# The last batch's first expert layer in two levels of seven products, with its factors streamed

## The chip, the cores and the metric

The kernel runs on one core of one Trainium2 chip, all in fp32. The metric is device microseconds (us) of one execution; three runs of the kernel before gave a median of 3222.79.

## The reference

`x` holds 4 batches of 2048 tokens of width 512. First comes a windowed attention with a layer norm before and after it, then a feed-forward layer whose weights are mixed per batch out of 8 experts:

```python
x = x + layernorm(attention(layernorm(x), w_qkv))      # windows of 128, 16 heads of 32, 3 windows of keys
h = layernorm(x)
# per batch of 2048 tokens here (the reference's own B, S, H, F, E names are kept)
g   = (relu(h @ gate_w1.T + gate_b1) @ gate_w2.T + gate_b2).mean(over the batch's tokens)   # 8 numbers
mW1 = W1 + sum_e g[e] * TW1[e]      # 2048 x 512
mW2 = W2 + sum_e g[e] * TW2[e]      # 512 x 2048
u   = gelu(h @ mW1.T + mb1)
out = x + layernorm(u @ mW2.T + mb2)
```

## The kernel before

The program runs in two stages. In the attention stage (up to about 1672 us) it walks 64 windows, and beside them it computes the gates. In the feed-forward stage it walks 16 blocks (`K`) of 512 tokens; batch `b` = K // 4, so blocks 12 to 15 are the last batch, called `DEEP`.

*Seven products for eight.* Both feed-forward layers cut each matrix into a 2 x 2 grid and compute 7 products of quarter matrices in place of 8 (Strassen's scheme in Winograd's form), with sums of the factors made before and sums of the results after. The names `A11, A12, S1, S2, S4, S3, A22` are the seven left factors made from the weights; the right factors come from the tokens.

- *First layer.* A block has four sets (`begin`, `middle`, `end`, c = 0, 2, 4, 6: two 128-row tiles of hidden units above and two below). Each set computes the seven products (`product`, L1023) into PSUM banks `X`, `Z`, `Y`, with 256 tokens as columns. The factors of a batch stay in SBUF for its four blocks (`w1_of`, loaded by `load_first` from `m1_d`).
- *Second layer.* `second` (`product2`, L1143) does the same with factors that are streamed from DRAM (`m2_d`) through six buffers `w2s` by `load_second`. For the last batch only, `second_deep` goes down one level more: each of the seven outer products is itself done as seven inner products (`inner`, L1308) of 128 columns, 49 in place of 64. The inner left factors come from `m3_d`. The inner right factors (`inner_right`) are made on DVE by `inner_sums` (four subtractions of 512 per outer product, L1233), one outer product ahead. Results go from PSUM to `y` by DVE adds (L1270) or ACT copies. POOL makes the outer right factors t1, b12 and t2 from the GELU results (L1105, L1106, L1111), and t3 at outer product 4 (L1345).
- *Mixing.* `mixer` is a generator (`blend`) that is advanced by hand at chosen places (`steps`, `next(blend)`). One step loads one expert's piece (512 KB, `exps`) three steps ahead and adds it into an accumulator on DVE (`scalar_tensor_tensor`, L155); after eight experts four DVE operations make the sums (L163 to L166), and stores put the factors into DRAM. It goes through batches, layers, eight chunks and eight experts in order, 576 steps in all. `inner_mixer` afterwards makes the inner sums of the last batch's second layer in 14 steps; it is advanced in block 11's second layer and in block 12's first.

How many steps each place takes is set by hand:

```python
step = mixing(*((2, 1, 1, 1) if c == 2 else (1, 1, 1, 1)))    # a set of the first layer
products2 = second(K, before, mixing(3, 2, 3, 2, 2, 3, 2), load_x1)
```

The order on each engine is the order of the program, and DMAs are issued from SP's queue, also in order. [...]

Of the kernel before, what the change touches and what calls it, by code (L numbers as in the profile page):

```python
# [34 lines left out]
def sandwich(ctx: ExitStack, tc: tile.TileContext, x, w_qkv, gw1, gb1, gw2, gb2, w1, b1, w2, b2, tw1, tb1, tw2, tb2, out):  # L35
# [23 lines left out]
    gw1_sb = const.tile([P, KC, D], F32, name="gw1_sb")  # L59
# [16 lines left out]
        for b in range(NB)  # L76
# [6 lines left out]
    m3_d = {b: dram.tile([P, 7, 8, PAIRS2, P], F32, name=f"m3d_{b}") for b in DEEP}  # L83
# [3 lines left out]
    order_deep = [A11, S1, A12, S3, S2, S4, A22]  # L87

# [17 lines left out]
    def mixer():  # L106

        todo = [(b, s, c, e) for b in range(NB) for s in range(2) for c in range(HC) for e in range(NX)]
        ets, accs = {}, {}
# [5 lines left out]
        def load(n):  # L115
            b, s, c, e = todo[n]
            base, exps = ((w1, tw1), (w2, tw2))[s]
            if e == 0:
                acc = mix.tile([P, 2, D], F32, tag="acc", name=f"acc_{b}_{s}_{c}")
                nc.sync.dma_start(acc, halves(base)[c])  # L120
                accs[b, s, c] = acc
            et = mix.tile([P, 2, D], F32, tag="exps", bufs=4, name=f"exps_{b}_{s}_{c}_{e}")
            nc.sync.dma_start(et, halves(exps[e])[c])
            ets[n] = et

        def store(b, s, c, acc, sums):
            rows = acc.rearrange("p h (q d) -> p h q d", d=Q)
            if s == 0:
# [5 lines left out]
            elif b in DEEP:  # L134
                for i, at in enumerate(((0, 7), (3, 6))[c % 2]):
                    cols = slice(i * P, (i + 1) * P)
                    nc.sync.dma_start(m3_d[b][:, A11 : A12 + 1, at, c // 2, :], rows[:, :, 0, cols])
                    nc.sync.dma_start(m3_d[b][:, S1 : S4 + 1, at, c // 2, :], sums[:, :, cols])
                    nc.sync.dma_start(m3_d[b][:, S3 : A22 + 1, at, c // 2, :], rows[:, :, 1, cols])
# [5 lines left out]
        for n in range(3):  # L145
            load(n)
        yield
        for n, (b, s, c, e) in enumerate(todo):
            if n + 3 < len(todo):
                load(n + 3)  # L150
            for f in late:
                f()
            late = []
            acc = accs[b, s, c]
            nc.vector.scalar_tensor_tensor(acc, ets.pop(n), g_all[b][:, e : e + 1], acc, ALU.mult, ALU.add)  # L155
            yield
            if e == NX - 1:
                del accs[b, s, c]
# [10 lines left out]
        for f in late:  # L169
            f()  # L170

    issued = {b: 0 for b in DEEP}

    def inner_mixer(b):

        todo = [(o, h) for o in order_deep for h in range(2)]
        loaded, late = {}, []

        def load(n):
            o, h = todo[n]  # L180
            two = slice(2 * h, 2 * h + 2)
            et = mix.tile([P, 4, 2, P], F32, tag="exps", bufs=4, name=f"inner_{b}_{o}_{h}")
            nc.sync.dma_start(et[:, :2], m3_d[b][:, o, 0:8:7, two, :])
            nc.sync.dma_start(et[:, 2:], m3_d[b][:, o, 3:7:3, two, :])
            loaded[n] = et

        def store(n, et):
            o, h = todo[n]
            two = slice(2 * h, 2 * h + 2)
            nc.sync.dma_start(m3_d[b][:, o, 1, two, :], et[:, 3])  # L190
            nc.sync.dma_start(m3_d[b][:, o, 2, two, :], et[:, 0])
            nc.sync.dma_start(m3_d[b][:, o, 4:6, two, :], et[:, 1:3])
            issued[b] = n + 1

        for n in range(2):
            load(n)
        yield
        for n in range(len(todo)):
            for f in late:
                f()  # L200
            if n + 2 < len(todo):
                load(n + 2)
# [1403 lines left out]
```

## Time and profile before

| | |
|---|---|
| median of three runs | 3222.79 us (3222.3 to 3224.71) |
| the profiled execution | 3220.89 us, span 3219.1 us |
| busy: PE, DVE, ACT, POOL | 3195.0, 2283.2, 1578.2, 676.9 us |
| blocks 1 to 11 of the feed-forward stage | 96.7 us each |
| blocks 12, 13, 14 | 94.0, 93.0, 93.1 us |
| block 15 and the end | 104.5 us |
| mean granted TensorE clock | 0.999 |

PE is the matmul engine, PEld its weight loads, DVE the vector engine, ACT the scalar engine, POOL GpSimd, SP the engine that issues the DMAs. In a row of the windows view the numbers are the stretch, its length, then the busy time of each engine with its instruction count, the granted clock, the DMA share and GB/s. A row of the timeline gives the start, the time taken (of all that are merged in it), the engine, the line and the operation; in brackets stands how long the engine was idle before, and what ended that. A row of waits reads: who waited for whom, us in total, times, longest. A matmul of fp32 appears as two instructions.

### The profile page before, as it was taken

What the parts mean: (1) busy time and instruction counts of PE and PEld (TensorE: products, weight loads), DVE (VectorE), ACT (ScalarE), POOL (GpSimd) and SP (SyncE); (2) the same over time, 40 slices, a digit from 0 to 9 for tenths busy, and PEclk for the clock granted to TensorE, in tenths of its full rate; (3) what the DMA queues carried; (4) which work ended last, traced back from release to release, by engine and by line L of the source; (5) the groups of instructions that cost most, each with busy time, mean ns of one, the idle gap of its engine ahead of it and who ended that gap; (6) DMA issues with size and microseconds to landing.
All of it is one profiled execution on the core that took longest, in us unless ns stands there. A gap on an engine that the chain in (4) does not pass through costs nothing.

```text
span 3219.1 us, 61654 instructions
## 1 busy us (share of the span) xinstructions
PE 3195.0 (99%) x23862; PEld 2695.0 (84%) x23862; DVE 2283.2 (71%) x3307; ACT 1578.2 (49%) x4332; POOL 676.9 (21%) x847
## 2 busy tenths in 40 slices
PE   9999999999999999999999999999999999999998
PEld 7788878788787887878768888888888888889998
DVE  5766666888998889888865665677757667554555
ACT  3777777777777777777761222112222112222222
POOL 0111111111111111110112332323322333322222
PEclk9999999999999999999999999999999999999999
DMA  2111112455555556554677889998999999874555
GB/s 87 52 59 54 41 60 80 134 185 170 195 194 164 176 176 202 192 183 149 213 276 277 310 308 346 359 336 326 313 329 364 336 328 321 305 248 162 193 187 171
DMA packets 363334, 688.88 MB, mean 214 GB/s; under 512 B 27161, under 2 KB 115353, under 8 KB 357026
## 3 DMA queue, kind: packets, MB, share of 16 engines
q1 hardware_dynamic: 363042, 684.94, 61.5%
q8 instruction: 189, 3.10, 0.4%
q14 instruction: 103, 0.84, 0.1%
HBM read 567.39 MB, written 117.44 MB: 213 GB/s over the span
## 4 chain that ended last, share of the span: by engine, by line
PE 95%; DVE 3%; DMA 1%; ACT 0%; POOL 0%; issue 0%; SPq 0%; POOLq 0%; DVEq 0%; ACTq 0%
PE pm L518 23%; PE px L1023 13%; PE ptp L686 11%; PE px L1143 7%; PE sc L649 7%; PE pz L1023 6%; PE po L707 5%; PE pz L1143 5%; PE py L1023 3%; PE px L1308 3%; PE py L1143 3%; PE py2b L1143 2%; PE pz L1308 1%; PE pm L582 1%; PE ptx L340 1%; PE pto L311 1%
## 5 line engine op out<-in xcount | busy, mean ns | idle before, releaser
L155 DVE SCALAR_TENSOR_TENSOR acc<-exps,g,acc 128x1024 f32<-128x1024 f32 x512 | 697.6, 1362 | 65.9 <-DMA exps<-in_tw 59.5
L658 DVE TENSOR_REDUCE nm<-sc 128x2 f32<-128x768 f32 (+1 forms) x512 | 449.1, 918 | 204.9 <-PE sc L649 199.9
L671 ACT ACTIVATE pr<-sc,nm 128x384 f32<-128x384 f32 (+1 forms) x1024 | 573.5, 593 | 11.1 <-DVE nm L658 11.0
L691 ACT COPY prT<-ptp 128x512 f32<-128x512 f32 x732 | 382.7, 594 | 278.7 <-PE ptp L686 278.3
L686 PEld LDWEIGHTS ptp<-ident,pr 128*128 128x128 f32 x2944 | 316.9, 140 | 102.0 <-issue 89.5
L686 PE MATMUL ptp<-ident,pr 128*128 128x128 f32 x2944 | 377.6, 277 | 0.0
L1060 ACT COPY py<-px 128x512 f32<-128x512 f32 x63 | 36.0, 571 | 661.4 <-PE px L1023 661.4
L1023 PE MATMUL px<-tT,w 128*128 128x256 f32 x1512 | 350.0, 379 | 0.6 <-DVE cpv L1083 0.6
L1023 PEld LDWEIGHTS px<-tT,w 128*128 128x128 f32 x1512 | 286.8, 190 | 40.1 <-DVE cpv L1083 1.0
L649 PE MATMUL sc<-k,q 32*128 32x384 f32 (+2 forms) x2816 | 242.8, 422 | 3.9 <-ACT pr L671 3.7
L671 ACT ACTIVATION_READ_ACCUMULATOR pr<-sc,nm 128x1 f32 x1024 | 236.3, 231 | 0.0
L1080 DVE TENSOR_TENSOR cpb<-pz,cpb 128x512 f32<-128x512 f32 x63 | 43.4, 689 | 268.6 <-PE pz L1023 239.0
L96 POOL TENSOR_SCALAR ve_b<-mv_b 128x1 f32<-128x1 f32 x64 | 42.9, 670 | 816.9 <-DVE mv_b L94 816.9
L707 PEld LDWEIGHTS po<-prT,v 128*32 128x32 f32 x5888 | 152.2, 110 | 50.9 <-ACT pr L671 24.6
L707 PE MATMUL po<-prT,v 128*32 128x128 f32 x5888 | 189.7, 275 | 0.2
L649 PEld LDWEIGHTS sc<-k,q 32*128 32x128 f32 x2816 | 118.4, 183 | 74.8 <-issue 53.7
L1143 PE MATMUL px<-w2s,u 128*128 128x256 f32 x784 | 175.1, 379 | 0.0
L1105 POOL TENSOR_TENSOR t<-u 128x512 f32<-128x512 f32 x60 | 81.7, 1362 | 433.9 <-ACT u L1035 433.9
L518 PE MATMUL pm<-xnT,wqkv 128*128 128x256 f32 x720 | 172.0, 382 | 0.0
L1143 PEld LDWEIGHTS px<-w2s,u 128*128 128x128 f32 x784 | 149.0, 190 | 20.3
L518 PEld LDWEIGHTS pm<-xnT,wqkv 128*128 128x128 f32 x720 | 132.0, 190 | 16.6
L1074 ACT COPY cpb<-px 128x512 f32<-128x512 f32 x63 | 36.9, 586 | 181.6 <-PE px L1023 181.6
(295 smaller groups left out, 5914.4 us busy)
## 6 DMA issues: line engine op xcount, KB each, us to landing
exps<-in_tw SPq DMA_DIRECT2D x512, 512.0 KB, 6.2
w2s<-m2d SPq DMA_DIRECT2D x168, 512.0 KB, 8.0
w2s<-m3d SPq DMA_DIRECT2D x84, 512.0 KB, 4.8
acc<-in_w SPq DMA_DIRECT2D x64, 512.0 KB, 6.5
x<-in_x SPq DMA_DIRECT2D x64, 256.0 KB, 4.0
m1d<-acc SPq DMA_DIRECT2D x64, 256.0 KB, 6.5
w<-m1d SPq DMA_DIRECT2D x16, 1024.0 KB, 7.7
fxT<-xTd SPq DMA_DIRECT2D x16, 1024.0 KB, 8.6
```

The costliest lines, as they stand in the source:

```text
L155: nc.vector.scalar_tensor_tensor(acc, ets.pop(n), g_all[b][:, e : e + 1], acc, ALU.mult, ALU.add)
L518: nc.tensor.matmul(bank[u not in chain][:, half, :], lhsT=a[:, kc, ts(half, P)], rhs=b[:, kc, :], start=(u not in (2, 3, 4) and half == kc ...
L649: nc.tensor.matmul(scs[r // 2][:, r % 2, col : col + nj * W], lhsT=q[rows, g, ts(W_ % WB, W)], rhs=k_of[kb][rows, g, j0 * W : (j0 + nj) * ...
L658: nc.vector.tensor_reduce(st["nm"][:, h : h + 2], scs[u][:, :, : nk * W], AX.X, ALU.max, negate=True)
L671: nc.scalar.activation(pr[:, : nk * W], scs[r // 2][:, r % 2, : nk * W], AF.Exp, bias=st["nm"][:, h : h + 1], accum_out=st["den"][:, h : h ...
L686: nc.tensor.transpose(pt[:, r, :], st["pr"][g * 4 + r][:, ts(j, W)], ident)
L691: nc.scalar.copy(prT, pt)
L707: nc.tensor.matmul(po[r * E : (r + 1) * E, n, :], lhsT=v_of[kb][:, jj, h * E : (h + 1) * E], rhs=prT[:, r, :], start=(j == 0), stop=(j == ...
L1023: nc.tensor.matmul(bank[:, f, :], lhsT=factor[:, f, kc * P : (kc + 1) * P], rhs=right[:, kc, :], start=(start and f == 0 and kc == 0), sto ...
L1105: nc.gpsimd.tensor_tensor(t1s[c], b12, us[c][:, :, :Q], ALU.subtract)
L1143: nc.tensor.matmul(bank[:, t, :], lhsT=right(c - c % 2)[:, c % 2, ts(t, P)], rhs=w[:, c % (HC // 2), :], start=(start and c == 0 and t == ...
L1308: nc.tensor.matmul(bank, lhsT=right(p), rhs=w[:, p, :], start=(start and p == 0), stop=True, skip_group_check=True,)
```

## The change

1. The last batch's first layer is computed in two levels too (`first_deep`): 7 outer products, each of 7 inner ones, with 128 weight rows as the stationary operand and 128 tokens as columns. The three inner-factor sets of outer products 1, 3 and 5 (`KEPT`) stay in SBUF for the batch; those of 0, 2, 4 and 6 are streamed again in every block through the six `w2s` buffers. The results of an outer product are added into the four blocks c11, c12, c21, c22 of the hidden matrix in SBUF, by DVE, ACT or POOL; GELU follows in place as a block is complete. `close`, called in the second layer's outer product 0, ends the last one and issues the last 12 GELUs and the eight POOL operations for b12 and t2.
2. The tokens' inner sums (`token_sums`) are made on DVE: part 0 for the next block at outer product 4 of the second layer, part 2 after product 0, part 1 after product 1. The first sums of the second layer (`prepare(0)`) are made after product 3 of the first.
3. Mixing follows a written plan (`mixing_plan`). For the second layer of batches 2 and 3 each expert piece is loaded once and added into two accumulators; batch 3's lie in the place of the gate weights, which are split into two tiles for that. The inner sums of both layers (28 steps) are part of the plan, loaded two steps ahead. Everything ends after product 1 of block 11's second layer. A chunk's stores are issued before the next load, not after it.
4. The step counts per set and product change, and `load_second` doesn't reach into the next block until that block's first layer has begun (`wanted`): two loads at each of the sets 2, 4 and 6.

```diff
+    order_first = [A11, A12, S2, S1, S4, S3, A22]
+    KEPT = (1, 3, 5)
...
+        def chunk(batches, k, c, between=()):
+            waiting = [x for x in todo if x[0] == "later"]
+            for e in range(NX):
+                todo.append(("mix", batches, k, c, e))
+                if e == 1 and waiting:
+                    todo.remove(waiting[0])
+                    todo.append(("sum", *waiting[0][1:]))
+            todo.append(("sum", batches[0], k, c))
+            for b in batches[1:]:
+                todo.append(("later", b, k, c))
+            todo.extend(("inner", *x) for x in between)
...
+        for b, k in ((0, 0), (0, 1), (1, 0), (1, 1), (2, 0)):
+            for c in range(HC):
+                chunk((b,), k, c)
+        for c in range(HC - 1):
+            chunk((2, 3), 1, c)
+        chunk((2,), 1, HC - 1)
+        chunk((3,), 1, HC - 1)
+        for c in range(HC):
+            chunk((3,), 0, c, again[1][2 * c - 2 : 2 * c] if c else ())
+        todo.extend(("inner", *x) for x in again[0])
...
+        def token_sums(K, part):
...
+            src, to = (
+                (xT.rearrange("p (i k) t -> p i k t", k=2)[..., :Q], xsum_of[K, 1][:, :, :2]),
+                (xT[:, 2:, Q:].unsqueeze(1), xsum_of[K, 1][:, :, 2:]),
+                (tT_of[K], xsum_of[K, 0]),
+            )[part]
+            g11, g12, g21, g22 = (src[:, :, k, j * P : (j + 1) * P] for k in range(2) for j in range(2))
+            a, b, c, d = (to[:, i] for i in range(4))
+            for args in ((a, g12, g11), (b, g22, a), (c, g22, g12), (d, g21, b)):
+                nc.vector.tensor_tensor(*args, ALU.subtract)
...
+            plan = [(c12, None), (c11, c12), (c21, c12), (c22, None), (c12, c12), (c21, c21), (c21, c21)]
...
+            def inner(j, n, bank, right, start=False):
+                w = weights_first(K, j, n)
+                for p in range(PAIRS2):
+                    nc.tensor.matmul(bank[:, p, :], lhsT=w[:, p, :], rhs=right, ...)
+
+            def emit(at, bank, out, other):
+                if other is None:
+                    nc.scalar.copy(out(at), bank)
+                else:
+                    add(out(at), bank, other(at))
...
+            def extra(j, at, engine):
+                if j == 3:
+                    add(c12(at), c21(at), c22(at), engine)
+                elif j == 5:
+                    add(c22(at), c22(at), c21(at), engine)
+
+            def tail(j, X):
+                right = tokens[j][1][:, 3, tokens[j][2]]
+                inner(j, 6, X, right)
+                released(j, 3)
+                emit((1, 0), X, *plan[j])
+                extra(j, (1, 0), nc.gpsimd if j == 3 else nc.vector)
...
+            for j in range(7):
...
+                inner(j, 0, X, raw(0, 0), True)
+                nc.scalar.copy(Y, X)
+                inner(j, 1, Z, sums[:, 0, at], True)
+                released(j, 0)
+                emit((1, 1), Z, out, other)
+                if tails:
+                    tails.pop()()
+                if j == 6:
+                    for c in range(0, HC, 2):
+                        nc.gpsimd.tensor_tensor(
+                            t1s["all"][:, c // 2], us[c][:, :, Q:], us[c][:, :, :Q], ALU.subtract
+                        )
+                inner(j, 2, X, sums[:, 1, at])
+                emit((0, 1), X, out, other)
+                gelu_some(j, 4)
+                inner(j, 3, Y, raw(1, 0))
+                released(j, 1)
+                emit((0, 0), Y, out, other)
+                extra(j, (0, 0), nc.gpsimd)
+                gelu_some(j, 2 if j < 6 else 0)
+                inner(j, 5, Z, raw(1, 1))
+                add(out((0, 1)), Z, out((0, 1)))
+                extra(j, (0, 1), nc.gpsimd)
+                gelu_some(j, 2 if j < 6 else 0)
+                inner(j, 4, X, sums[:, 2, at])
+                released(j, 2)
+                add(out((1, 1)), X, out((1, 1)))
+                extra(j, (1, 1), nc.vector)
+                if j == 0:
+                    token_sums(K, 2)
+                if j == 1:
+                    token_sums(K, 1)
+                if j == 3:
+                    next(products2)
+                tails.append(lambda j=j, X=X: tail(j, X))
+                yield
+
+            def close():
+                tails.pop()()
+                for f in (*acts[6], *gelus(K, 1, 0)):
+                    f()
+                for c in range(0, HC, 2):
+                    p, b12, b22 = c // 2, us[c][:, :, Q:], us[c + HC][:, :, Q:]
+                    nc.gpsimd.tensor_tensor(b12, b22, b12, ALU.subtract)
+                for c in range(0, HC, 2):
+                    p, b22 = c // 2, us[c + HC][:, :, Q:]
+                    nc.gpsimd.tensor_tensor(t2s[p // 2][:, p % 2], b22, t1s["all"][:, p], ALU.subtract)
...
@@ second_deep
+                if o == 4 and not last_block:
+                    token_sums(K + 1, 0)
...
                 if o == 0:
-                    end(*closing)
+                    closing.pop()()
...
@@ the loop over blocks
-                elif K == 0 or (k == NBLK - 1 and b + 1 < NB):
-                    step = mixing(0, 1, 0, 1)
+                elif k == NBLK - 1 or K == 0:
+                    step = mixing(*((0, 1, 0, 1) if K in (0, 11) else (1, 1, 1, 1)))
                 else:
-                    step = mixing(*((2, 1, 1, 1) if c == 2 else (1, 1, 1, 1)))
-                if K // NBLK in DEEP and k == 0:
-                    step = lambda: next(inner, None)
+                    step = mixing(*((2, 1, 1, 1) if c == 2 or (c == 4 and PAIRED <= K < 2 * NBLK) else (1, 1, 1, 1)))
...
+                counts = (3, 3, 3, 3, 3, 3, 3) if PAIRED <= K < 2 * NBLK else (3, 2, 3, 2, 2, 3, 2) if b < 2 else (2,) * 7
+                products2 = second(K, before, mixing(*counts), load_x1)
...
+                if K + 1 == DEEP[0] * NBLK:
+                    if j == 1:
+                        assert next(blend, 0) == 0
+                    if 1 < j < 5:
+                        load_kept(j - 2)
+                    if j == 5:
+                        token_sums(K + 1, 0)
```

## The prediction

> **What bounds the kernel now.** I read the page's busy line first, then TensorE's waits in the last four blocks (those of batch 3, the only batch whose matmuls change), then their windows, the chain, and the timeline around one block's second layer.
>
> ```profile
> PE 3195.0 (99%) x23862; PEld 2695.0 (84%) x23862; DVE 2283.2 (71%) x3307; ACT 1578.2 (49%) x4332; POOL 676.9 (21%) x847
> ```
>
> ```profile
> PE px L1308 <- DVE y L1270: 1.5, 5, 0.8
> ```
>
> ```profile
> 2834.50:2928.50 94.00, 92.97 (x617) 86.53 (x617) 61.88 (x123) 24.97 (x59) 27.73 (x27) 1.00 0.72 249
> 2928.50:3021.50 93.00, 92.79 (x618) 86.54 (x617) 46.70 (x97) 24.98 (x59) 27.02 (x30) 1.00 0.50 173
> ```
>
> ```profile
> 2860.37 1.73 PE py L1023 x8
> ...
> 2889.41 1.79 PE px L1308 x16
> ```
>
> TensorE (PE) is busy for 99% and waits for others for 1.5 us in the last 385 us. So time goes only if PE has less to do, and comes back if PE is made to wait. The windows are blocks 12 and 13 (us, PE, PEld, DVE, ACT, POOL, clock, DMA share, GB/s). The chain gives both matmul prices: eight 256-column instructions take 1.73 us (the first layer, L1023), eight 128-column ones 1.79/2 = 0.893 us (the second layer by eighths, L1308).
>
> The price of waiting stands in the timeline, DVE then POOL:
>
> ```profile
> 2883.47 1.76 DVE L1233 TENSOR_TENSOR inner_right<-u 128x512 f32<-128x512 f32 x1
> 2885.15 1.75 DVE L1233 TENSOR_TENSOR inner_right<-u,inner_right 128x512 f32<-128x512 f32 x1
> 2887.03 0.27 DVE L1270 TENSOR_TENSOR y<-px,mb 128x128 f32<-128x128 f32 x1
> 2888.76 0.68 DVE L1233 TENSOR_TENSOR inner_right<-t 128x512 f32<-128x512 f32 x1
> 3002.49 2.69 DVE L1233 TENSOR_TENSOR inner_right<-t,inner_right 128x256 f32<-128x256 f32 x2
> ```
>
> ```profile
> 2883.17 1.51 POOL L1105 TENSOR_TENSOR t<-u 128x512 f32<-128x512 f32 x1 [1.90 <-ACT u L1035]
> 2884.76 1.60 POOL L1106 TENSOR_TENSOR u<-u,u 128x512 f32<-128x512 f32 x1
> 2886.32 1.72 POOL L1111 TENSOR_TENSOR t<-u,t 128x512 f32<-128x512 f32 x1
> 3000.61 5.71 POOL L1345 TENSOR_TENSOR u<-u,t 128x512 f32<-128x512 f32 x4 [18.65 <-PE pz L1308]
> ```
>
> The same DVE operation, 512 wide with both inputs in SBUF, takes 0.68 us alone and 1.75 while POOL works: it stands until POOL's operation (1.27 alone) has ended. One that reads PSUM (2887.03) isn't held. A 256-wide pair at 3002.49 took 2.69 instead of 0.75.
>
> **The PE term.** The first layer of a block is 4 sets x 7 products x 8 instructions: 28 x 1.7275 (6.91 us for 32 in the chain) = 48.4 us. By eighths it is 49 groups of 8 at 0.893 = 43.8. That is 4.6 less per block, 18.4 in four. Both layers ideally take 92.1 now; block 13 takes 93.0, so 0.9 is lost already (the junction of the layers, and the fifth outer product). I keep it. Block 12 loses 1.0 more, where the inner sums still run in its first layer; these now end in block 11: -1.0.
>
> **DVE's work.** The new first layer has 34 adds of 512 from PSUM for 8 now (0.69 each: +17.9), 3 SBUF adds (+2.1) and the token sums, four each of 512, 256 and 128 (0.69, 0.42 by the weight sums' row, 0.28: +5.6). DVE goes from 46.7 to 72 us of some 92: not the bound by its sum. But it works in order, and PE needs certain adds within one product (7 groups, 6.25 us). So I walked one block's queues by hand, each operation at the duration above:
>
> 1. Products 3 to 4. Behind product 3's last add DVE has one extra add and the four sums for the second layer's first product, 0.69 + 4 x 0.65 = 3.3 us, before it can empty product 4's Z bank (0.69). With 0.2 to reach DVE and 0.6 for the add itself that is 4.8 us; PE comes back to Z after 5 groups, 4.5 us. Stall 0.3. POOL meanwhile runs three extra adds; each that comes in between holds DVE for up to 1.27, so up to 2.4. I take 1.4: between the ends, one hold.
> 2. Product 6. POOL's four differences for t1 (5.1 us) stand beside a DVE extra add that is ahead of the add freeing X. 0 to 1.0; I take 0.6.
> 3. Second layer, outer products 0 and 1. Now three POOL operations fall here (2883.17 to 2888.04); after the change eight do (b12 and t2 of all four pairs, 10.2 us), since all the last GELUs come at the end. The next eight inner sums of DVE stand beside them, four at 1.7 instead of 0.65: +4.2 us. Of that some 3 are covered, as sums are made one outer product ahead. 0 to 2.5; I take 1.0.
> 4. Outer product 4, in blocks 12 to 14. Four token sums (256 wide) are put ahead of this product's adds, exactly where POOL's four L1345 operations run and where PE already stalls now:
>
> ```profile
> 3005.84 1.16 PE L1308 MATMUL px<-w2s,inner_right 128*128 128x128 f32 x8 [0.18 <-DVE y L1270]
> ```
>
> Alone they are 4 x 0.33 = 1.3 us, and one hold of about 1 us more before POOL ends at 3006.3. There is no slack, so 2.0 goes to PE. From 0.5 (DVE catches up behind it) to 5.0 (each held at 1.3, as at 3002.49).
>
> These are the edits that speak against the saving. [...]
>
> **Edits with no cost, and their cover.** *Mixing.* 39 DVE steps in blocks 4 to 6 instead of 34, 5 x 1.45 = 7 us more on 66 to 70 busy of 96.7; 33 and 37 instead of 25 in blocks 3 and 7, 12 to 17 more on 54. PE there waits for nobody, and each bank's add has a product (6.9 us) to come. If that cover fails, up to 1 us in each of four blocks; a gain is excluded beyond the 1.9 us of PE waits in blocks 1 to 11. *Loads.* 56 expert loads of 512 KB fall away in the pairs (29 MB); the streamed factors add 4 x 7 tiles of 256 KB per block, also 29 MB. That is 7.3 MB per block of some 92 us, +80 GB/s on 173 at a DMA share of 0.50, about block 12's 249 GB/s at 0.72, which held PE up in no row. Six tiles are ahead (over 10 us of PE) and land in 4.8. They share SP's queue with the output stores, which wait for DVE's adds at products 1 and 2; the same lead covers that, and the kept product 1 reads no stream. *Stores ahead of loads.* In the mixer SP now waits for the weight sums (4 x 0.42 to 0.67 us) before the next load; three loads are ahead, so DVE at worst waits where PE doesn't. *Block 11 to 12.* The last inner sums, kept loads and first token sums end in block 11's second layer, where DVE has 47.1 us of work in 96.7; 0 to 3 us. *Split gate weights.* The same matmuls; nothing.
>
> **The sum.** Against the profiled execution's span of 3219.1: -18.4 - 1.0 + 4 x (1.4 + 0.6 + 1.0) + 3 x 2.0 = -1.4, so 3217.7. The execution's own time is 3220.89, 1.8 above its span, and the median of the runs 3222.79, 1.9 above that: 3217.7 + 3.7 = 3221.4, say 3221. With all unknowns at their low ends: -19.4 + 4 x 0.3 + 3 x 0.5 = -16.7, to 3206; if the 0.9 per block went too, 3203. At their high ends, with the mixing's 4 and the 3 at block 12: -19.4 + 4 x 5.9 + 3 x 5 + 7 = +26, to 3249.
>
> **The rivals.** *PE keeps most of its saving* (0.36): the holds fall on POOL or into DVE's idle 20 us per block. At 0.5 each for items 1 to 3 and 1.0 for item 4: -19.4 + 6 + 3 = -10.4, 3212. For it: DVE is far from full, and a hold of 1.2 is less than two groups. Against: at 3005.84 one hold already reached PE. *The port decides against it* (0.19): the eight POOL operations and the token sums cost their bounds, 2.5 and 5.0, the rest as taken: -19.4 + 4 x 4.5 + 3 x 5 = +13.6, 3236. It ends slower once the new stalls pass 19.4/4 = 4.9 us per block, and by over 0.2% from (19.4 + 6.4)/4 = 6.5. For it: the three operations in the rows stretch two sums to 1.75. Against: in block 12 that stretch alone cost PE no wait in any row. *The blend isn't ready* (0.05): block 12 waits for its streamed or kept factors, one load chain of store, load and sum, three times 5 to 6 us: 3221 + 10 to 15. *Stalls eat the saving* (0.40) is the forecast.
>
> **How the numbers follow.** 0.2% (6.4 us) is about what a measurement of this kernel can tell from no change. The forecast case lies within it; the first rival is faster; the other two are slower: 0.36, 0.40, 0.24. The forecast case's own range is 3216 to 3228. The range of 8 in 10 takes in most of the first rival and part of the second, 3207 to 3235.
>
> **What would show it.** Matmuls at L1023 down by 896 (4 x 4 x 56), and 1568 new ones of 128 columns at 0.893 us per eight; if these cost more, the PE term is wrong. Blocks 12 to 14 at 92 to 95 us and 15 at 90 to 92 of PE; 88 to 90 each would be the first rival, 96 or more the second. PE waits on DVE of about 3 us per block in the first layer's products 4 and 6 and the second's outer products 1 and 4, with DVE operations at 1.2 to 1.8 us beside POOL's; if PE waits but DVE is not beside POOL there, the cause is DVE's order alone. Blocks 1 to 11 at 96.7 each; longer, and the mixing isn't free. A PE wait on DMA at w2s would make the load reasoning wrong.

## The result: 1.1% slower, and the profile after

The changed kernel took 3258.95 us (3255.42 to 3262.51) against 3223.11 us for the kernel before on the same chip, a ratio of 1.0111 [1.0093, 1.0128]. The predicted 3221 (3207 to 3235) is missed by 38 us. The profiled execution of after took 3262.51 us, span 3260.7, 41.6 more than before's 3219.1. Where the 41.6 lie, by the starts of the blocks' first matmuls:

| part | before | after | difference |
|---|---|---|---|
| up to block 0 | 1672.6 | 1674.2 | +1.6 |
| blocks 0 to 2 | 290.6 | 291.7 | +1.1 |
| block 3 | 96.7 | 106.1 | +9.4 |
| blocks 4 to 7, each | 96.7 | 96.7 | 0 |
| blocks 8, 9, 10 | 96.7, 96.7, 97.6 | 103.5, 103.6, 99.4 | +15.5 |
| block 11 | 96.7 | 96.7 | 0 |
| blocks 12, 13, 14, 15 | 94.1, 93.0, 93.0, 93.2 | 98.3, 96.4, 98.2, 95.3 | +14.8 |
| from the last matmul on | 11.5 | 10.7 | -0.8 |

So there are two losses: 25 us in blocks 3 and 8 to 10, where no matmul changed, only the mixing and the order of the loads, and 15 us in the last batch, from which the prediction took 19.4 us off.

In after's kernel the first layer's product stands in L1075 (by eighths in L1264), the second layer's in L1372 (by eighths in L1538). A mixing step is L245, the adds of a first-layer set are L1132 and L1135, those of the first layer by eighths L1258, the inner sums L1462 and the token sums L1227.

The busy line of after's page, and then TensorE's waits in two stretches, 1676 to 2862 us (blocks 0 to 11) and 2862 to the end (who waited for whom, us in total, times, longest):

```profile
PE 3199.7 (98%) x24534; PEld 2717.5 (83%) x24534; DVE 2418.7 (74%) x3527; ACT 1589.7 (49%) x4344; POOL 707.9 (22%) x867
```

```profile
PE px L1075 <- DVE cpv L1135: 15.7, 5, 6.7
PE py L1075 <- ACT py L1112: 4.3, 2, 3.7
...
PE px L1538 <- DVE y L1481: 12.1, 8, 2.5
PE pz L1264 <- DVE u L1258: 7.4, 4, 1.9
PE px L1264 <- DVE u L1258: 1.4, 4, 0.4
```

Before's TensorE waited 1.5 us in the last 385 us, and in blocks 0 to 11 for no more than 0.68 us at a time. After has 20.7 us of waits ahead of block 12 and 21.5 from there on. PE's busy time is 4.7 us higher than before although its work fell by 896 instructions at L1075 and 1568 half-wide ones took their place: some of the work ran slower. The windows (us, PE, PEld, DVE, ACT, POOL, granted clock, DMA share, GB/s) show where. First blocks 3 and 8 of before, then blocks 3, 8, 9 and 13 of after:

```profile
1963.17:2059.87 96.70, 96.70 (x450) 85.12 (x449) 53.90 (x66) 22.56 (x48) 29.99 (x28) 1.00 0.94 344
2446.64:2543.33 96.69, 96.69 (x449) 85.11 (x448) 69.48 (x83) 22.50 (x48) 32.62 (x30) 1.00 0.94 335
...
1965.87:2071.93 106.06, 99.36 (x449) 86.73 (x448) 65.17 (x76) 22.68 (x48) 29.82 (x27) 0.97 0.97 359
2458.71:2562.23 103.52, 98.91 (x449) 86.14 (x448) 69.32 (x86) 22.42 (x48) 29.04 (x32) 0.98 0.96 332
2562.23:2665.80 103.57, 99.42 (x449) 86.79 (x448) 64.61 (x90) 22.36 (x48) 29.31 (x28) 0.97 0.93 315
2960.14:3056.52 96.38, 90.62 (x786) 89.66 (x785) 76.56 (x138) 27.61 (x62) 34.66 (x35) 0.98 0.71 243
```

The clock column was 1.00 in blocks 0 to 14 of before. Blocks 3, 8 and 9 of after stand at a DMA share of 0.93 to 0.97, and stood at 0.93 and 0.94 before, so they were nearly full already. In blocks 12 and 13 the share is 0.70 and 0.71, and TensorE waited 0.6 us in all for a streamed factor in the last batch: these are not what is short there.

**The wait in block 3.** DVE's rows of the timeline, and under them PE's:

```profile
2002.55 1.28 DVE L1650 TENSOR_TENSOR fx<-fx,y 128x512 f32<-128x512 f32 x2
2016.03 2.60 DVE L245 SCALAR_TENSOR_TENSOR acc<-exps,g,acc 128x1024 f32<-128x1024 f32 x2 [12.20 <-DMA exps<-in_tw]
2018.55 0.68 DVE L1132 TENSOR_TENSOR cpb<-pz,cpb 128x512 f32<-128x512 f32 x1
...
2020.35 0.68 DVE L1135 TENSOR_TENSOR cpv<-px,cpv 128x512 f32<-128x512 f32 x1
...
2021.08 3.35 PE L1075 MATMUL px<-tT,w 128*128 128x256 f32 x7 [6.70 <-DVE cpv L1135]
```

DVE stands 12.2 us at a mixing step whose expert piece hasn't landed. The add that empties PE's bank takes 0.68 us and needs no DMA, but it is behind that step in DVE's queue. The view names DVE as what PE waited for; the DMA behind it is in the bracket of the DVE row. The chain gives what came ahead of that piece:

```profile
1991.77 6.49 DMA out<-fx
...
2003.62 12.32 DMA exps<-in_tw
```

SP's queue stood 5.5 us at a load (L1639) until a store of outputs (`out<-fx`) had landed; the loads of factors and the expert piece came after it, and the piece landed 12.3 us later, where the median in block 3 is 8.1. The wait for that store isn't the cause by itself: in blocks 4 and 5 of after it was 4.3 us, and TensorE waited for nothing there.

The wait of 4.2 us in block 9 has the same form. Those of blocks 8 and 10 have not. The longest of block 8 is for ACT:

```profile
2474.29 1.52 ACT L1645 ACTIVATE y<-y,shift,rs_d 128x512 f32<-128x512 f32 x2 [7.15 <-POOL shift L1644]
...
2476.34 3.63 PE L1075 MATMUL py<-fxT,w 128*128 128x256 f32 x8 [3.66 <-ACT py L1112]
```

ACT's copy stands behind an operation of the layer norm (L1645), whose statistics DVE made late: from 2462.6 to 2475 DVE worked without a pause through five mixing steps, four weight sums and the statistics. So DVE is behind with its steps there, with no piece missing at that moment. In block 10 DVE stood 3.2 us at a piece for an inner sum and then made eight operations of such sums ahead of the add.

**The waits in the last batch.** Product 4 of the first layer in block 13, DVE, POOL and PE:

```profile
2988.33 1.75 DVE L1462 TENSOR_TENSOR inner_right<-u,inner_right 128x512 f32<-128x512 f32 x1
2990.01 0.68 DVE L1258 TENSOR_TENSOR u<-pz,u 128x512 f32<-128x512 f32 x1
...
2987.84 1.70 POOL L1258 TENSOR_TENSOR u<-u 128x512 f32<-128x512 f32 x1 [1.90 <-ACT u L1275]
...
2990.74 1.16 PE L1264 MATMUL pz<-fxT,w2s 128*128 128x128 f32 x8 [1.81 <-DVE u L1258]
2991.73 1.71 PE L1264 MATMUL px<-xsum,w2s 128*128 128x128 f32 x8
2993.24 1.91 PE L1264 MATMUL px<-tT,kept 128*128 128x128 f32 x8
2994.95 1.26 PE L1264 MATMUL pz<-xsum,kept 128*128 128x128 f32 x8
```

One of DVE's four sums takes 1.75 us in place of 0.68 beside POOL's operation (2987.84 to 2989.54), the add behind it comes late, and PE waits 1.81 us: the prediction's item 1. What it did not have is in the next rows: eight instructions start 1.51 and 1.71 us apart in place of 0.89. The windows of that stretch have the clock beside it:

```profile
2991.40:2994.80 3.40, 3.40 (x21) 3.40 (x20) 1.86 (x3) 0.00 (x0) 0.00 (x0) 0.58 0.09 19
2994.80:2998.20 3.40, 3.40 (x30) 3.40 (x30) 1.48 (x3) 1.26 (x3) 0.00 (x0) 0.92 0.44 151
```

The granted clock falls to one half for 3.41 us, from 3.0 us after the wait began (by the trace's clock record, from 2991.95 on). The windows agree: 0.42 and 0.08 of 3.40 us are 1.7 us, half of 3.41, and they are lost on top of the wait.

Item 4, the token sums at the second layer's outer product 4, in the same block:

```profile
3038.37 1.28 DVE L1227 TENSOR_TENSOR xsum<-fxT 128x256 f32<-128x256 f32 x1
3039.68 0.43 DVE L1227 TENSOR_TENSOR xsum<-fxT,xsum 128x256 f32<-128x256 f32 x1
...
3033.81 5.56 POOL L1577 TENSOR_TENSOR u<-u,t 128x512 f32<-128x512 f32 x4 [14.54 <-PE pz L1538]
...
3041.23 1.16 PE L1538 MATMUL px<-w2s,inner_right 128*128 128x128 f32 x8 [2.52 <-DVE y L1481]
```

### The profile page after: what moved, and what is told of

Read it like the earlier page. It is cut to its first block, busy times and chain, and to the rows that moved or that the text cites. A ratio compares the mean times of both kernels' runs of the same rounds, so it can differ in the third digit from the quotient of the medians.

```text
span 3260.7 us, 63452 instructions
## 1 busy us (share of the span) xinstructions
PE 3199.7 (98%) x24534; PEld 2717.5 (83%) x24534; DVE 2418.7 (74%) x3527; ACT 1589.7 (49%) x4344; POOL 707.9 (22%) x867
## 4 chain that ended last, share of the span: by engine, by line
PE 86%; DVE 7%; DMA 5%; issue 1%; ACT 1%; SPq 1%; POOL 0%; DVEq 0%; POOLq 0%; ACTq 0%
PE pm L570 22%; PE ptp L738 11%; PE px L1075 7%; PE px L1372 7%; PE sc L701 7%; PE po L759 5%; PE pz L1372 5%; PE pz L1075 4%; PE px L1264 3%; PE py L1372 2%; PE px L1538 2%; PE py2b L1372 2%; DVE inner_right L1462 2%; PE py L1075 2%; DMA exps<-in_tw 2%; DVE acc L245 1%
## 5 line engine op out<-in xcount | busy, mean ns | idle before, releaser
L245 DVE SCALAR_TENSOR_TENSOR acc<-exps,g,acc 128x1024 f32<-128x1024 f32 x512 | 693.6, 1363 | 100.9 <-DMA exps<-in_tw 97.1
L1112 ACT COPY py<-px 128x512 f32<-128x512 f32 x47 | 26.8, 570 | 574.5 <-PE px L1075 574.5
L1075 PE MATMUL px<-tT,w 128*128 128x256 f32 x1128 | 265.0, 383 | 15.7 <-DVE cpv L1135 15.7
L1075 PEld LDWEIGHTS px<-tT,w 128*128 128x128 f32 x1128 | 216.2, 192 | 47.7 <-DVE cpv L1135 18.0
L1372 PE MATMUL px<-w2s,u 128*128 128x256 f32 x784 | 176.5, 381 | 0.0
L1372 PEld LDWEIGHTS px<-w2s,u 128*128 128x128 f32 x784 | 150.2, 192 | 20.9
L1157 POOL TENSOR_TENSOR t<-u 128x512 f32<-128x512 f32 x44 | 62.5, 1420 | 322.7 <-ACT u L1087 322.7
L1132 DVE TENSOR_TENSOR cpb<-pz,cpb 128x512 f32<-128x512 f32 x47 | 32.4, 690 | 118.4 <-PE pz L1075 118.4
L98 POOL TENSOR_SCALAR ve_d<-mv_d 128x1 f32<-128x1 f32 x62 | 22.3, 360 | 395.5 <-DVE mv_d L96 395.5
```

Of the source, the lines that this page charges most:

```text
L245: nc.vector.scalar_tensor_tensor(acc, et, g_all[b][:, e : e + 1], acc, ALU.mult, ALU.add)
L1075: nc.tensor.matmul(bank[:, f, :], lhsT=factor[:, f, kc * P : (kc + 1) * P], rhs=right[:, kc, :], start=(start and f == 0 and kc == 0), sto ...
L1372: nc.tensor.matmul(bank[:, t, :], lhsT=right(c - c % 2)[:, c % 2, ts(t, P)], rhs=w[:, c % (HC // 2), :], start=(start and c == 0 and t == ...
```

## The experiments

Two questions were open: what makes the mixing's loads late, and whether the last batch's stalls are the ones named, with the half clock as the rest. Block times in this section come from each kernel's profiled execution; they are those of one execution each, and the executions of a kernel that stalls lie up to 12 us apart (e3). The groups of experiments ran on different chips, where the kernel before took 3221.90 to 3225.48 us, so kernels are compared by their ratios to it.

### The order of the DMAs

After issues a chunk's stores ahead of the next load, and `wanted` holds back the factor loads of the next block. `e1_ungated` frees that gate everywhere but at block 8, `e2_loads_first` puts the load first again, `e7_both_orders` does both, and `e8_orders_on_before` puts both new orders into the kernel before.

```diff
# e1                                   # e2
-                if K and c:           -                flush()
+                if K == 8 and c:                        ahead()
...                                    +                flush()
```

> The next block's first six factor tiles are again loaded as the buffers come free at the end of the block before, not two at each set (block 8 alone keeps the gate, as its factors aren't stored before). Theory A (the w2s loads put between an expert load and the x1 load make the expert piece late): block 3 loses its 11 us, so about 3252; block 8 keeps its 13.6. Theory B (block 3 simply asks the DMA for too much, 16 steps beside the next batch's factor loads): block 3 stays 105 or more, total within 3 us of 3259. Theory C (stores issued ahead of loads): no change.

> In a mixing step the next expert load is issued ahead of the last chunk's stores again. Theory C: SP's wait for the weight sums delayed the expert load; blocks 3 and 8 lose most of their 11 and 13.6 us, total about 3235. Theories A and B: within 3 us of 3259, the blocks as they were.

> Both orders on SP's queue undone: first factor tiles loaded early (but for block 8) and expert loads ahead of stores. If the queue's order causes the waits, blocks 3 and 8 to 11 are within 2 us of 96.7 each, total about 3238. If it is the amount loaded (theory B) or the place of the steps (D), at least one of blocks 3, 8 to 11 keeps a wait of 3 us or more, total above 3245.

> The kernel before with these two orders alone: factor tiles two at each set, chunk stores ahead of the next expert load. If the orders cause the waits, blocks 8 to 10 show PE waits of 2 us or more, total 3228 to 3240. If not, within 3 us of 3223.

Measured: e1 3249.82 us, 1.0077 [1.0048, 1.0107]; e2 3255.59, 1.0095 [1.0066, 1.0125]; e7 3251.94, 1.0089 [1.0055, 1.0124]; e8 3224.02 against 3223.56, 1.0004 [0.9993, 1.0015]. Freeing the gate gained some 11 us by the ratios (1.0111 and 1.0077, whose intervals overlap), but the waits only changed place: block 9 fell from 103.6 to 99.1 and block 11 rose from 96.7 to 103.8. With both orders as before, blocks 3, 8, 9 and 11 still took 103.6, 98.6, 103.3 and 102.8. With both new orders in the kernel before, blocks 3 to 11 stayed at 96.7 or 96.8. The orders are not the cause by themselves. (The expectations count 11 us for block 3 and 13.6 for block 8; the table above has 9.4, and 6.8 for block 8 alone.)

### How many steps, and where

Block 3 has 33 mixing steps in place of 25. `e3_steps` gives it 25 again and puts the eight into the sets of blocks 4 to 7. `e5_last_set` takes no steps in a block's last set and more in its second layer.

```diff
# e3, for blocks 3 and 7
-                    step = mixing(*((0, 1, 0, 1) if K in (0, 11) else (1, 1, 1, 1)))
+                    step = mixing(*((0, 1, 0, 1) if K in (0, 3, 11) else (2, 1, 1, 1) if K == 7 and c in (2, 4) else (1, 1, 1, 1)))
# and for blocks 4 to 6
-                    step = mixing(*((2, 1, 1, 1) if c == 2 or (c == 4 and PAIRED <= K < 2 * NBLK) else (1, 1, 1, 1)))
+                    step = mixing(*((2, 1, 1, 1) if c == 2 or PAIRED <= K < 2 * NBLK else (1, 1, 1, 1)))
```

> Block 3 makes 2 mixing steps per set instead of 4, as before the change; the 8 steps are made in blocks 4 to 7, whose loads serve two batches. Theory B: block 3 back at 96.7, blocks 4 to 7 still 96.7, total about 3248. Theories A and C: block 3 improves by less than half of its 11 us. Block 8 unchanged in all.

> No mixing step stands in the last set (c = 6) of a block's first layer; its steps (4, or 2 in blocks 0 and 11) go to the second layer's seven products. Nothing else changes, the DMA has the same to do. Theory D (an expert piece that lands late holds the mixing step, and in DVE's queue the last set's two adds stand behind it, which PE needs within 2 us; elsewhere there is slack): the waits of 1 to 7 us in blocks 3, 8, 9 and 10 vanish, blocks 1 to 11 near 96.7 each, total 3259 - 24 = about 3235. Theory B (too much to load in those blocks): the waits turn up in the second layer, total within 6 us of 3259.

Measured: e3 3261.79, 1.0114 [1.0070, 1.0159]: no gain. But block 3 is back at 96.7, and block 4 now takes 108.2 with a wait of 8.4 us. e5 3264.47, 1.0128 [1.0078, 1.0179]: blocks 3, 4, 8 and 11 took 101.7, 102.5, 106.5 and 104.6. The place within a block doesn't decide, and the waits go where the steps go. But neither the number of steps nor the bytes tell by themselves which block stalls: block 4 of e3 moved 32.0 MB with a wait of 8.4 us, and block 4 of before 32.2 MB with none.

### The stalls of the last batch

`e4_tokens` makes the next block's token sums at outer product 2 instead of 4, where POOL's four operations (L1577) don't stand. `e6_split` adds to that: the sums for the second layer's first product come in two halves, behind first-layer products 3 and 4.

```diff
-                if o == 4 and not last_block:
+                if o == 2 and not last_block:
# e6 besides
-                if j == 3:
+                if j in (3, 4):
                     next(products2)
...
-            run(dve, 4)
+            run(dve, 2)
+            yield
+            run(dve, 2)
```

> The next block's first token sums are made at outer product 2 of the second layer instead of 4, away from POOL's four operations. If they cost what the profile says, the 2.5 us wait at outer product 4 falls to about 0.3 in blocks 12 to 14, and with it the 3.4 us at half clock that follow it in two of the three: blocks 12 to 14 shorter by 2 to 4 us each, total about 3250. Rival (POOL's operations alone hold DVE there, wherever the token sums are): the wait stays above 1.5 us, total within 2 us.

> Token sums at outer product 2, and of the four sums for the second layer's first outer product two are made after product 3 and two after product 4 of the first layer. If the 1.8 us wait at product 4 comes from DVE's four sums in one piece, it falls to 0.5 or less, blocks 12 to 15 lose 1.5 us each and any half-clock time behind it (1.7 each): against the run with the token sums moved alone 6 to 10 less, about 3238, blocks 12 to 15 at 91 to 91.5. Rival (POOL's holds decide): the wait stays over 1.2, or moves to product 5.

Measured: e4 3246.65, 1.0065 [1.0042, 1.0088]; e6 3234.32, 1.0036 [1.0023, 1.0050]. In e4 the waits of 2.52 us became 0.18, and blocks 12 to 14 went to 94.7, 92.7 and 94.5. In e6 the waits of 1.81 went too, and blocks 12 to 15 took 90.9, 90.6, 90.8 and 90.9, 10 us under before's 373.3 in all. All waits of TensorE that are left in e6 from block 12 on, and the window of its block 13:

```profile
PE px L1540 <- DVE y L1481: 5.1, 8, 1.1
PE px L1264 <- DVE u L1258: 1.4, 4, 0.4
```

```profile
2950.42:3041.05 90.63, 88.98 (x786) 88.02 (x785) 74.86 (x138) 27.61 (x62) 34.23 (x35) 1.00 0.76 260
```

The clock is 1.00. The half clock can also be priced without any edit to these blocks: after's blocks 13 and 14 have the same code and nearly the same waits (5.8 and 5.9 us), and 13 took 96.4 us with one half-clock stretch, 14 98.2 with two. So 1.8 for one, and 1.7 by the clock record (half of 3.41). After has six of these stretches in blocks 12 to 15: 10 us.

### A level plan of the steps

With e6's last batch as a base, `f1_plan` gives block 3 25 steps, block 4 36, blocks 5 to 7 (two accumulators to a load) 44 each and blocks 8 to 10 29 each; after had 33 in block 3, 39 in 4 to 6, 37 in 7 and 31 in 8 to 10. `f2_plan_loads_first` is f1 with e2's edit; `f3_plan_more` has 46 in blocks 5 to 7 and 27 in 8 to 10.

```diff
-                counts = (3, 3, 3, 3, 3, 3, 3) if PAIRED <= K < 2 * NBLK else (3, 2, 3, 2, 2, 3, 2) if b < 2 else (2,) * 7
+                counts = (3, 2, 3, 2, 2, 3, 2) if b == 0 else (4, 3, 4, 3, 4, 3, 3) if b == 1 else (2, 2, 2, 2, 2, 2, 1)
...
```

> Starting from the run with the token sums and the split: mixing steps are taken out of the blocks whose expert loads serve one batch and put where they serve two. Block 3 has 25 steps again (33), block 4 36 (39), blocks 5 to 7 44 each (39, 39, 37), blocks 8 to 10 29 each (31). Theory B (the DMA can't deliver the pieces in time in blocks 3 and 8 to 10): block 3 at 96.7, blocks 5 to 7 still at 96.7, blocks 8 to 10 lose at least half of their 14 us of delay; total 3234 - 10 - 7 to 14 = 3210 to 3217, below the kernel before. Rival (any denser mixing stops PE): blocks 5 to 7 take over the waits, total over 3230.

> The same with expert loads issued ahead of a chunk's stores. If the order on SP's queue adds to the lateness in the full blocks, blocks 8 to 10 lose another 2 us or more; if only the amount counts, within 3 us of f1_plan.

> Blocks 5 to 7 with 46 steps each, blocks 8 to 10 with 27. By theory B blocks 8 to 10 come within 1.5 us of 96.7 each, and 3 us below f1_plan in all, unless DVE in blocks 5 to 7 (some 46 x 1.4 + 18 = 82 of 96.7 us) begins to stop PE there.

Blocks 6 and 7 of f1, with 44 steps each:

```profile
2255.98:2352.68 96.70, 96.70 (x450) 85.12 (x449) 80.40 (x93) 22.59 (x48) 34.73 (x30) 1.00 0.86 290
2352.68:2457.87 105.19, 99.82 (x449) 87.01 (x448) 74.64 (x88) 22.68 (x48) 29.71 (x27) 0.97 0.96 357
```

Measured: f1 3236.88, 1.0044 [1.0027, 1.0060]; f2 3236.13, 1.0038 [1.0023, 1.0053]; f3 3253.13, 1.0091 [1.0076, 1.0106]. Block 3 at 96.7 for good. But in f1 block 7, which like block 3 also loads the next batch's first-layer factors (7.3 MB), took 105.2, and in f3, with two steps more, 117.7. Block 6 above has more of DVE's work and no wait, but it moved 28.1 MB against 37.5 in block 7 (33.2 in block 3 of before, 38.1 of after). So in blocks 3 and 7, which load factors too, the loads decide and not DVE's steps. Blocks 8 and 9 stayed at 104 in f1. f2 settles the order of stores and loads once more: no difference.

### Block 7, the inner sums and their buffers

`f4_seven` is f1 with 37 steps in block 7 and 31, 31 and 32 in blocks 8 to 10. On it, `f5_inner_late` puts the second layer's 14 inner sums behind chunks 6 and 7 instead of two behind each chunk, and `f6_inner_slots` issues the load that follows into an inner sum's buffer one step later.

```diff
# f5
-            chunk((3,), 0, c, again[1][2 * c - 2 : 2 * c] if c else ())
+            chunk((3,), 0, c, again[1][7 * c - 42 : 7 * c - 35] if c > 5 else ())
# f6: prev is the kind of the step before
-            while loads and len(ets) < (3 if loads[0][0] == "inner" else 4):
+            while loads and len(ets) < (3 if "inner" in (loads[0][0], prev[0]) else 4):
```

> The kernel f1 with block 7 at 37 mixing steps in place of 44; blocks 8 to 10 get 31, 31 and 32. Theory 'a last block of a batch cannot take more' (it also loads the next batch's 7.3 MB of factors): block 7 goes from 105.2 back to 96.7 us, so about 8 us less than f1, 3228 to 3230. Rival 'the sets' sum is what counts and the wait only moves on': block 8 or 9 grows by as much as 7 falls, and the time stays at 3236. Both expect blocks 8 and 9 still at about 103 to 104.

> f4 with the second layer's 14 inner sums put after chunks 6 and 7 of the last mixing (seven each) instead of two after each of chunks 1 to 7, so that blocks 8 and 9 hold none. Theory 'inner sums hold up the queue' (their three buffers' loads and stores in short rows, and an expert load that stands in SyncE's queue until an inner store has landed): blocks 8 and 9 return to 96.7 to 98 from 103 to 104, block 10 or 11 becomes the dense one and loses up to 8; 3215 to 3228. Rival 'the wait in 8 and 9 comes from something else there' (the steps' own number, the gate's tiles as accumulators): 8 and 9 stay above 102.

> f4 in which the step after an inner sum loads no expert piece further than three ahead; the load into the inner sum's buffer is issued one step later, when the inner store has had a step's time to land. The amount of traffic is the same. Theory 'the wait for the buffer in SyncE's queue': blocks 8 and 9 fall from about 103.5 to under 99, and SyncE's waits for the inner stores at the expert load, 7 of up to 8 us, shrink to under 3 us each. Theory 'the short rows of the inner traffic themselves': 8 and 9 stay within 1.5 us of f4.

Measured: f4 3232.42, 1.0029 [1.0018, 1.0040]; f5 3251.20, 1.0086 [1.0071, 1.0101]; f6 3232.32, 1.0026 [1.0017, 1.0036]. Block 7 came down to 97.7; blocks 8 to 11 took 102.4, 97.0, 104.2 and 103.8. f6 is equal to f4, but its edit had next to nothing to remove: from 2440 to 2870 us SP's queue waited 2.7 us for inner stores at the expert loads in f4, and 2.6 in f6. A wait of this size is not the cause. In f5 blocks 8 and 9, without inner sums, still took 101.4 and 101.8: the theory of f5 falls as the whole cause. But blocks 10 and 11, with all of them, took 112.0 and 107.8, so the inner sums do cost. What they change in the loads is in the DMA part of the profile, here for block 9 of before and then of after:

```profile
DMA packets 17281, 31.97 MB, mean 331 GB/s; under 512 B 1194, under 2 KB 4906, under 8 KB 17147
...
DMA packets 21903, 32.63 MB, mean 315 GB/s; under 512 B 1507, under 2 KB 12176, under 8 KB 21768
```

By the same view of blocks 8, 9 and 10, after moved 98.9 MB in 306.5 us and before 96.3 in 291.0: 2.7% more bytes at 323 GB/s in place of 331, with the 16 DMA engines about as full (0.93 to 0.96 against 0.93 to 0.95). The packets under 2 KB rose from 15065 to 38092. By the shapes in the code, expert pieces in rows of 2 KB gave way to inner sums in rows of 1 KB. That the short rows lower the rate is a reading of these counts; no run changed them alone.

### Lighter blocks 8 to 11

`g1_inner_in_12` is f4 with seven inner sums moved to the end of the plan, six of them in block 12's first layer, and 29 steps in blocks 8 to 10. `g2_level` takes 45 in blocks 5 and 6 and 26, 29 and 30 in 8 to 10.

> f4 with the last 7 inner sums of the second layer moved out of blocks 8 to 11: one ends block 11's mixing, six go one by one into block 12's first layer; blocks 8 to 10 take 29 steps each. Theory 'the sixteen DMA engines are full': share times length is 98, 91, 94 and 97 us in blocks 8 to 11 of f4, blocks stall from about 95, and 7 of the 28 inner sums are some 14 us of the four blocks' engine time: all four fall to about 97 or less, the time to 3214 to 3222, block 12 grows by 0 to 4 from DVE's 11 us of extra sums. Rival 'something else in the last mixing steps': blocks 8, 10 and 11 stay at 102 or more, 3230.

> g1 with one step more in each of blocks 5 and 6 (45) and 26, 29 and 30 steps in blocks 8, 9 and 10, block 8 having the fullest DMA engines. 'The sixteen DMA engines are full': block 8 at 97 to 98, the sum 1 to 4 us under g1, 3212 to 3220. Rival 'DVE's steps count': blocks 5 and 6, where DVE is busy for 75 to 81 us, lose 2 or more each and the gain is gone.

Measured: 3240.80, 1.0051 [1.0036, 1.0066], and 3241.90, 1.0053 [1.0036, 1.0070]; both expectations are missed, by 19 and 22 us. Blocks 9 and 10 did fall, to 96.7 and to 97.7 or 97.6. Block 8 took 102.5 and 101.0. And block 11 took 108, block 12 97.3 and 98.7: in g1 PE waited 2.6 and 4.5 us for streamed factors at block 12's start, where the last batch's first loads now share SP's queue with inner stores. The expectation had not priced that.

### Spread once more

`h1_spread` is f4 with 38 steps in block 4, 45 in 5 and 6, 37 in 7 and 29, 31 and 30 in 8 to 10; `h2_seven_light` has 38 and 45 in blocks 4 to 6 too, but 33 in block 7 and 31, 32 and 31 in 8 to 10.

```diff
# h2 against f4, blocks 7 to 10
                 if K == 7:
-                    counts = (3, 3, 3, 3, 3, 3, 3)
+                    counts = (3, 2, 3, 2, 2, 3, 2)
+                if K == 9:
+                    counts = (2, 2, 2, 2, 2, 3, 3)
                 if K == 10:
-                    counts = (2, 2, 2, 2, 2, 3, 3)
+                    counts = (2, 2, 2, 2, 2, 3, 2)
```

> f4 with the steps spread again: 38 in block 4, 45 in 5 and 6, 37 in 7, 29, 31 and 30 in 8 to 10. Theory 'a block stalls when its loads come late, and that depends on how much it and the block ahead of it ask of the DMA engines': block 4 stays at 96.7 (share 0.89 with 36 steps), block 8 falls from 102.4 to 98 to 100, 10 and 11 from 104 to 97 to 100; 3213 to 3224, so at or below before. Rival 'the last part of the plan stalls wherever it lies': the sum of blocks 8 to 11 stays within 3 us of f4's 407, 3229 to 3233.

> As h1, but 33 steps in block 7 (which also loads 7.3 MB of the next batch's factors) and 31, 32 and 31 in 8 to 10. If block 8 stalls because block 7 leaves a backlog of loads, it comes down to under 98 here although it has two steps more than in h1; if its own steps decide, it is at 101 to 104 as in f4, which has 31 there too. Blocks 9 to 11: about f4's.

Measured: h1 3221.82 against 3222.75, 1.0000 [0.9992, 1.0009]; h2 3220.72, 0.9994 [0.9985, 1.0003]. Both are level with the kernel before. h1's time is as expected, but its block 8 rose where it should have fallen. Each has one block left that loses over 9 us. Block 8 of h1, then blocks 8 and 10 of h2:

```profile
2450.05:2556.48 106.43, 98.92 (x450) 86.13 (x449) 71.85 (x88) 22.50 (x48) 30.66 (x32) 0.98 0.92 317
...
2447.09:2543.78 96.69, 96.69 (x450) 85.12 (x448) 61.50 (x80) 22.68 (x48) 29.25 (x29) 1.00 0.95 323
...
2641.37:2747.53 106.16, 99.72 (x449) 86.96 (x448) 68.32 (x98) 22.47 (x48) 31.96 (x28) 0.97 0.91 307
```

Block 8 takes 96.7 with 31 steps where block 7 has 33, and 102 to 106 with 31 and 29 where block 7 has 37 (f4, h1). f4 and h2 are the closest pair: 161 steps in blocks 4 to 7 in both, so block 8 begins at the same place of the plan and has the same 31 steps. Yet 29 expert loads are issued within block 8 in f4 and 24 in h2 (33.9 MB against 31.3): in f4 the block does what block 7 left undone. So its wait is a backlog from the block ahead. Why block 10 loses in h2 isn't shown: it has 31 steps there, and lost nothing with 31 in e1 and e7.

## Why the prediction was wrong, step by step

**The step that failed** is "Edits with no cost, and their cover: mixing", with at most 1 us in each of four blocks. Measured were 25 us in blocks 3 and 8 to 10, and blocks 8 to 10, where steps of the inner sums take the place of expert steps, are not in that paragraph at all. It costed DVE's steps by DVE's time, which held: block 3 has DVE busy for 65 of 106 us. It did not cost the load that every step carries. Block 3 moved 33.24 MB before at a DMA share of 0.94, as before's windows show, and 38.07 MB after. By estimate, at before's 344 GB/s the 4.8 MB more are 14 us of a channel that had some 6 left (0.06 of 96.7); the block grew by 9.4. The paragraph on loads argued with what fell away, 29 MB in the pairs, but in blocks 4 to 6 (share 0.92 to 0.93 before, 0.80 to 0.86 after), not in block 3. The mixing's cover for a bank's add, a product of 6.9 us, is that of the second layer; in the first, where after's long waits stand, a product takes 1.73. The sentence "DVE at worst waits where PE doesn't" is wrong: DVE works in order, and the adds that PE needs stand behind its waiting step (in block 3 DVE waited 12.2 us for the piece, and PE 6.70 for the add behind it). e3, f1 and f3 show that in blocks 3 and 7 the steps with their loads decide, f4 and h2 that block 8 pays for block 7, and e8 and f2 that the two orders don't decide.

**The stalls of the last batch** were right in kind and place, and nearly in size. Taken were 1.4, 0.6, 1.0 and 2.0 us for items 1 to 4; the waits measured are 1.81, 0.35, 1.1 and 2.52 per block, 21.5 in the four blocks against 18 taken. ("About 3 us per block" among the signs doesn't fit these items, which add up to 5.0.) e4 removes item 4 by moving the token sums away from POOL's operations, e6 item 1 by cutting the four sums in two; how much of item 1 is POOL's hold (1.75 - 0.68 us) and how much DVE's order wasn't separated.

**A term was missing**: TensorE's half clock behind such a wait, 6 x 1.7 = 10 us in blocks 12 to 15, and some 8 us in blocks 3, 8 and 9, where PE is busy for 2.2 to 2.7 us more than before with the same matmuls. No view of before shows one: in the four blocks of the last batch it has no wait over 0.81 us.

**The PE term** was a little high. PE is busy for 92.80 us in block 13 before and 88.98 in e6, 3.8 less where 4.6 was taken, though eight 128-wide instructions do cost 0.89. Where the other 0.8 go is open. With these: -4 x 3.8 - 1.0 + 21.5 - 0.7 (waits of before in these blocks that the 1.0 doesn't hold) + 10.2 = +14.8, and the last batch lost 14.8.

**The rivals.** "The port decides against it" forecast blocks 12 to 14 at 96 or more and got 96.4 to 98.3, though part of that is the half clock, not DVE's holds. No run shows a port as such; the rows of block 13 show a sum of DVE at 1.75 us for 0.68 beside an add of POOL at 1.70 for 1.25. And before's block 12 does have a wait of PE behind its two stretched sums: 0.81 us at 2887.36. "PE keeps most of its saving" needed the edits of e6: its 88 to 90 per block are 90.6 to 90.9 there. "The blend isn't ready" was not seen in after; g1 made it happen. No PE wait for streamed factors over 0.6 us came up in after's last batch, so that part of the loads held.

**Still open**: the demand at which a block begins to stall, and so most of the 15.5 us in blocks 8 to 10. A full channel alone doesn't tell: f1's block 9 lost 7.5 us with 31.4 MB at a DMA share of 0.89, h1's block 10 nothing at 0.96, and before's block 9 nothing with 32.0 MB at 0.93. f5 took the short rows of the inner sums out of blocks 8 and 9, which still lost 5 us each. The order in which SP's queue waits and DVE's own delay could have a part; no run took one of these away alone.

## What to carry to other kernels

Cost a moved step with everything it brings along, its DMA before its arithmetic, and against the DMA share of the block that it goes to: block 3, at 0.94, could not take 4.8 MB more, however idle DVE was. On an engine that works in order, as DVE did here, an operation that may wait for a load (12.2 us in block 3) should not stand ahead of the one that frees TensorE's bank (an add of 0.68). And a TensorE wait of about 2 us cost nearly twice its length here when the clock fell after it (1.81 us and 1.7 more in block 13), so to make such waits short can be worth more than the waits themselves.

## What the runs showed of the hardware

By after's clock record, TensorE's granted clock fell to one half in the feed-forward stage seven times for 3.41 us (six of them in blocks 12 to 15, one in block 8) and twice for 6.83 (blocks 3 and 9), each time beginning 2.2 to 4.8 us after a wait of TensorE began. All four waits of 1.81 to 1.94 us were followed by it, two of the three of 2.51 to 2.52 and all three of 3.66 to 6.70; the one of 2.42 and those up to 1.44 us were not. Before's waits in that stage were 0.81 us at most, and its clock stayed full there up to the last matmul. What sets these lengths no run shows.
